# Second graph stream: late arrival of the last hidden state, and its next input normalised in two halves

## Chip, cores and metric

The kernel runs on one core of a Trainium2 chip. The metric is device time in microseconds (us) of one execution. Engines are named as in the profile: PE is TensorE's matmul, PEld its weight load, DVE is VectorE, ACT is ScalarE, POOL is GpSimd, SP is the queue that issues most DMAs.

## What is computed

The reference takes 16 graphs of 1024 nodes with 128 features each, a 0/1 adjacency per graph, and runs two residual blocks. The first block, where the change lies, is a gated graph network of 4 layers:

```python
h = relu(layernorm(x))
for i in range(4):
    m = einsum('bjn,bjd->bnd', adj, h @ weight[i])
    h = gru_cell(m, h, w_ih[i], w_hh[i], b_ih[i], b_hh[i])
x = x + h * mask
```

The second block is a 4-layer graph convolution with batch normalisation over `relu(layernorm(x))`. It is not touched.

## The kernel before

**Two streams.** The first block handles graphs in pairs: stream `sa` (the first stream) has the even graphs, stream `sb` (the second) the odd ones. While one stream sums over its adjacency, the other goes through its gates, so that PE always has matmuls. `half_step(one, two)` (L1032) is that unit: PE first does `two.gate_step(0)` and `two.gate_step(1)` (L955, the two halves of 512 nodes), then `one.agg_step(0)` and `one.agg_step(1)` (L525, 32 matmuls). Eight half-steps take a pair through a layer-by-layer cycle, and a loop (L1201) alternates `half_step(sa, sb)` and `half_step(sb, sa)`. `clock` counts them.

I number the half-steps of a cycle from the one in which `sb` finishes its graph:

| half-step | gates | aggregation |
|---|---|---|
| 0 | `sb`, layer 3 (then `sb` finishes) | `sa`, layer 0 of its next graph |
| 1 | `sa`, layer 0 | `sb`, layer 0 |
| 2 | `sb`, layer 0 | `sa`, layer 1 |
| 3 | `sa`, layer 1 | `sb`, layer 1 |
| 4 to 6 | and so on | |
| 7 | `sa`, layer 3 (then `sa` finishes) | `sb`, layer 3 |

**Gates.** For each half: six f32 matmuls into four PSUM tiles `g_r`, `g_hn`, `g_xn`, `g_z`, of which there is one set (so the second half may only write `g_z` after the first half's `z` has been read out); then on ACT sigmoid `r` (L981), tanh `r` (L987), sigmoid `z` (L988), and on DVE `r` (L982, L983) and the new `h` (L992 or L994, then L995, L996).

**Between layers.** The new `h` must come back turned (features by nodes to nodes by features). DVE turns 32x32 blocks (`t_h`, L711), SP writes them to DRAM (`cross_h`, L591, one DMA per half) and reads them back (`n_h`, L598, four DMAs per half). `split_back` (L898) then makes the aggregation's weights in two parts: ACT casts the high part `ghw` (L905, "hi" below, hi0 and hi1 for the halves) and DVE subtracts to get the low part (L906, "lo"). PE's aggregation wants hi0 first, lo0 two matmuls later, and hi1, lo1 only half-way.

**After a graph.** When a stream finishes (`finish`, L1001), the next graph's normalised input `y` takes the same road (`t_in`, `cross_in`, `h_in`), and so does the last `h` (`t_out`, `cross_out`, back into the two halves of `h`: `parts`, eight DMAs of L598). DVE then adds it to `x` and takes the sums of the layer norm (`tail_sums`, L717: L732, L658, L659). The next graph's `y` (`next_blocks`, L818) is made on ACT in eight blocks of 128 columns (L674, `y_in`).

**What sets the order.** Three engine orders are written by hand in this stage: PE, POOL and SP run in the order of the code. ACT and DVE are ordered by a scheduler that works with its own estimates, held by `behind(...)` (L761), which keeps instructions after named ones. Work that isn't of the current half-step is put on an agenda: `at(clock, place, what)` (L1025), run by `due(place)` (L1028). The place `"ins"` stands at the head of a half-step, `"outs"` between the two gate steps, `"gap"` between the two halves of the aggregation.

**The adjacency's transposes.** During the same cycle the adjacency blocks are transposed for the second block: POOL casts a row block to bf16 (L609, into two buffers), SP issues a DMA transpose (L610), a few per half-step (`feed.some`).

Of the kernel before, what the change touches and what calls it, by code (L numbers as in the profile page):

```python
# [8 lines left out]
F32 = mybir.dt.float32  # L9
# [7 lines left out]
P = 128  # L17
# [324 lines left out]
def exact_path(  # L342
# [22 lines left out]
    B, N, C = x.shape  # L365
    L = g_weight.shape[0]
    NB = N // P
    NH = N // HALF
    BH = HALF // P
# [28 lines left out]
    def turned_tile(name):  # L398
        return keep.tile([P, NB, N], BF16, tag="adjT", name=name, bufs=1)
# [134 lines left out]
    with ExitStack() as st:  # L534
        work = st.enter_context(tc.tile_pool(name="work", bufs=2))
# [58 lines left out]
        def exchange_in(d, t):  # L594

            src = d.rearrange("(t r) (s x) -> s r t x", t=4, s=4)
            for s in range(4):
                nc.sync.dma_start(t[s * 32 : (s + 1) * 32, :].rearrange("r (t x) -> r t x", t=4), src[s])  # L598
# [7 lines left out]
        def transpose_rows(b, row, j, adjT):  # L606

            t = work.tile([P, N], BF16, tag="half1", name=f"half{b}_{j}", bufs=2)
            nc.gpsimd.tensor_copy(t, row.bitcast(F32))  # L609
            return lambda: nc.sync.dma_start_transpose(adjT[:, :, j * P : (j + 1) * P], t)  # L610

        def transposes(batches):

            for b, rows in batches:
                adjT = turned_tile(f"adjT{b}")
                ahead = transpose_rows(b, rows[0], 0, adjT)
                for j in range(NB):
                    go = ahead
                    if j + 1 < NB:
                        ahead = transpose_rows(b, rows[j + 1], j + 1, adjT)  # L620
                    go()
                    yield j
                nc.gpsimd.dma_start(adjT_d[b].rearrange("k p n -> p k n"), adjT)
                yield NB
# [47 lines left out]
        def norm_blocks(xt, y, nt, ks):  # L672
            for k in ks:
                nc.scalar.activation(  # L674
                    y[:, k * P : (k + 1) * P], xt[:, k, :], AF.Relu, bias=nt[3][:, k, :], scale=nt[2][:, k, :]
                )
# [29 lines left out]
        def blocks_out(src, name):  # L706

            return [half_out(cross_tile(f"t_{name}_{hf}"), src, hf, name)[0] for hf in range(NH)]
# [39 lines left out]
        def last_tail(b, xt, hT):  # L748
            nt = tail_sums(b, xt, hT)
            y = y_mid(b) if b + 1 < B else xt.rearrange("p k c -> p (k c)")  # L750
            store_xmid(b, xt)

            def rest():
                norm_apply(xt, y, nt)
                store_ymid(b, y)

            return rest
# [3 lines left out]
        def behind(*inss):  # L761

            es = ExitStack()
            for ins in () if written[0] else inss:
                es.enter_context(tc.issue_after(ins.ins))
            return es

        class Stream:
# [47 lines left out]
                norm_factors(self.next_norm)  # L816

            def next_blocks(self):  # L818
                self.next_y = work.tile([P, N], F32, tag=f"y{self.tag}", name=f"y_in{self.b + 2}", bufs=1)
                norm_blocks(self.next_x, self.next_y, self.next_norm, range(NB))  # L820

            def plan(self, n, tail=None):

# [177 lines left out]
            def finish(self):  # L1001

                if self.i < L:
                    return
                args = self.b, self.xt, self.hT
                self.b, self.i = self.b + 2, 0
                if self.b >= B:
                    self.rest = last_tail(*args)
                    return
                ins = self.take()  # L1010
                h_in = self.hT
                outs = blocks_out(args[-1], f"out{args[0]}")
                parts = [args[-1][:, hf * HALF : (hf + 1) * HALF] for hf in range(NH)]

                def arrive(ds, ts):
                    for d, t in zip(ds, ts):
                        exchange_in(d, t)

                at(clock[0] + 1, "ins", lambda: arrive(ins, [h_in[:, :HALF], h_in[:, HALF:]]))
                at(clock[0] + 1, "outs", lambda: arrive(outs, parts))  # L1020
                self.plan(clock[0], (*args, parts))

        clock = [3]

        def at(n, place, go):  # L1025
            agenda.setdefault((n, place), []).append(go)

        def due(place):  # L1028
            for go in agenda.pop((clock[0], place), ()):
                go()  # L1030

        def half_step(one, two, gated=None, halfway=None):  # L1032

            feed.next_step()
            one.split = []
            if one.i == 0:
                two.fetch()
            due("ins")
            if one is sb and one.i == 0 or written[0] and one is sa:
                feed.jobs = transposes([(s.b, s.rows) for s in (sa, sb)])  # L1040
            if one.i > 0:
                one.split_step()
                two.fetch()
                feed.some(2)
            two.gate_step(0)
            two.half_away(0)
            two.first_four()
            if feed.full or (clock[0], "mid") in agenda:

                pace = small.tile([P, 1], F32, tag="pace", name=f"pace{clock[0]}")  # L1050
                nc.gpsimd.tensor_copy(pace, two.new[:, :1])
                feed.store()
                due("mid")
            due("outs")
            one.split_back(0, two.last_act, two.mid_dve)
            one.split_back(1, two.last_act, two.mid_dve)
            if one.i > 0:
                feed.some(1)
            two.gate_step(1, None, one.split)
            two.half_away(1)  # L1060
            with behind(two.first_act):
                due("late")
            if one.i == 0:
                feed.some(1)
            two.last_four()
            if gated:
                gated()
            if one.i == 0:
                with behind(two.last_m):
                    one.split_step()  # L1070
            one.agg_step(0)
            if halfway:
                halfway()
            with behind(two.last_act, two.last_dve, *one.split):
                due("gap")
            feed.some(NB if written[0] and one is sa else 1)
            one.agg_step(1)
            two.finish()
            clock[0] += 1

        sa, sb = Stream(0), Stream(1)
        every = {getattr(mybir.EngineType, e) for e in ("PE", "DVE", "Activation", "Pool", "SP")}
        with tc.tile_pool(name="prep", bufs=1) as prep, tc.manual_schedule(engines=every):
# [107 lines left out]
            sa.plan(0)  # L1191
            sb.plan(1)
            half_step(sa, sb, looks, lambda: turn_layer(prep, w_g, 1))
            join_layer(1)
            half_step(sb, sa, None, lambda: turn_layer(prep, w_g, 2))
            join_layer(2)
            turn_layer(prep, w_g, 3)
            join_layer(3)
        with tc.manual_schedule(engines={getattr(mybir.EngineType, e) for e in ("PE", "Pool", "SP")}):
            written[0] = False  # L1200
            for s in range(2, B // 2 * L):  # L1201
                half_step(sa, sb)
                half_step(sb, sa)
            assert not agenda, sorted(agenda)
            sb.gate_step(0)
            sb.gate_step(1)
            with tc.issue_after(sb.last_act.ins):
                sa.rest()
            sb.finish()
# [11 lines left out]
    work = ctx.enter_context(tc.tile_pool(name="work2", bufs=2))  # L1221
# [211 lines left out]
    for b in range(B):  # L1433
# [3 lines left out]
        for n0, n in pieces(b):  # L1437
# [3 lines left out]
            tag = turns[count % len(turns)]  # L1441
# [60 lines left out]
```

## Time and profile before

| | us |
|---|---|
| median of 3 runs (1797.73 to 1798.45) | 1797.83 |
| the profiled execution | 1797.0 |
| its span | 1795.1 |
| PE busy in the span | 1762.7 |
| granted TensorE clock, mean | 0.997 |

The span is what the profile shows; the 1.9 us beside it lie before and after. The first block takes the stretch from about 50 to 1160 us, the second the rest. PE is busy nearly everywhere, so what counts is where PE stands idle. The timeline of PE names each idle time of this stage with what ended it; the starts of the 32-matmul aggregations (L525) give the length of each half-step. Undisturbed, they start 17.57 us apart.

### The profile page before, as it was taken

To read this page: it belongs to the slowest core of one execution; us is meant where nothing else is said; L and a number is where in the kernel's file an instruction comes from. 1 tells how busy PE (TensorE), PEld (TensorE's weight loads), DVE (VectorE), ACT (ScalarE), POOL (GpSimd) and SP (SyncE) were. 2 spreads that over 40 slices of the span, in tenths; PEclk is the share of its full clock that TensorE was granted. 3 is DMA by queue.
4 is the path that set the end of the run, shared out by engine and by line. 5 is a ranking of instruction groups with operands and counts; after the bars stand their busy time and mean duration, and the time that the engine had idled before them with its cause. 6 is when DMAs were issued, how large, how long until landed. Compare 5 with 4: busy or idle time off the path is not lost.

```text
span 1795.1 us, 22286 instructions
## 1 busy us (share of the span) xinstructions
PE 1762.7 (98%) x6742; PEld 1194.2 (67%) x6742; DVE 1259.4 (70%) x2307; ACT 1108.3 (62%) x1717; POOL 389.0 (22%) x417
## 2 busy tenths in 40 slices
PE   9999999999999999999999999999999999999997
PEld 6555555565566555656555655677778888888886
DVE  7567867877776776877686766676666666666665
ACT  5346557466556555655655645477777767768765
POOL 3213423332332331422332333010100000000010
PEclk9999999999999999999999999999999999999999
DMA  6447777676676766766866767778866565757666
GB/s 252 113 127 263 190 206 245 197 214 212 213 208 217 230 192 196 255 201 175 284 175 187 246 197 211 270 270 309 280 220 246 205 247 207 255 214 251 230 227 255
DMA packets 363968, 399.11 MB, mean 222 GB/s; under 512 B 159820, under 2 KB 240496, under 8 KB 363840
## 3 DMA queue, kind: packets, MB, share of 16 engines
q1 hardware_dynamic: 343088, 322.54, 56.9%
q0 software_dynamic: 20224, 74.80, 11.5%
q8 instruction: 55, 0.90, 0.2%
q14 instruction: 73, 0.60, 0.1%
q10 hardware_dynamic: 528, 0.26, 0.0%
HBM read 266.95 MB, written 96.99 MB: 203 GB/s over the span
## 4 chain that ended last, share of the span: by engine, by line
PE 81%; DMA 5%; DVE 5%; ACT 4%; issue 2%; SPq 2%; DVEq 0%; ACTq 0%
PE pm L525 20%; PE pc_m L525 13%; PE g_z L969 10%; PE g_r L969 9%; PE pc_g_z L525 6%; PE pc_g_r L525 6%; PE g_xn L969 5%; PE g_hn L969 5%; PE hw_c L500 4%; DMA cross_in<-t_in 1%; ACT y_in L674 1%; SPq L598 1%; DMA stage<-in_adj_dram 1%; DMA cross_h<-t_h 1%; PE pw_g_hn L1302 1%
## 5 line engine op out<-in xcount | busy, mean ns | idle before, releaser
L525 PE MATMUL pm<-row,ghw 128*128 128x512 f32 x2048 | 505.3, 403 | 10.7 <-ACT ghw L905 10.6
L525 PEld LDWEIGHTS pm<-row,ghw 128*128 128x128 f32 x2048 | 384.3, 188 | 123.1 <-issue 26.3
L525 PE MATMUL pc_m<-wide,chw 128*128 128x512 f32 x1024 | 246.0, 395 | 0.0
L609 POOL CAST half<-row 128x1024 bf16<-128x1024 f32 x128 | 147.9, 1163 | 329.0 <-DMA adjT<-half 314.2
L525 PEld LDWEIGHTS pc_m<-wide,chw 128*128 128x128 f32 x1024 | 190.4, 188 | 42.3 <-issue 4.3
L988 ACT ACTIVATE z<-g_z,brz 128x512 f32<-128x512 f32 x128 | 87.5, 684 | 172.6 <-PE g_z L969 172.3
L525 PE MATMUL pc_g_r<-wide,chw 128*128 128x512 f32 x464 | 186.9, 403 | 0.3 <-ACT chw L502 0.3
L578 POOL CAST row<-stage 128x1024 fp32r<-128x1024 f32 x112 | 132.9, 1196 | 241.0 <-DMA stage<-in_adj_dram 194.9
L525 PE MATMUL pc_g_z<-wide,chw 128*128 128x512 f32 x464 | 181.0, 390 | 0.0
L982 DVE SCALAR_TENSOR_TENSOR r<-g_hn,vecs,r 128x512 f32<-128x512 f32 x128 | 95.1, 743 | 121.4 <-ACT r L981 76.6
L944 ACT COPY m<-pm 128x512 f32<-128x512 f32 x128 | 68.5, 587 | 151.6 <-PE pm L525 151.6
L1234 DVE CAST wide<-block 128x1024 fp32r<-128x1024 bf16 x160 | 109.9, 692 | 73.2 <-PE pc_m L525 48.3
L1234 DVE CAST wide<-packed 128x1024 fp32r<-128x1024 bf16 x160 | 110.2, 691 | 72.0 <-PE pc_g_z L525 53.9
L987 ACT ACTIVATE r<-r,vecs 128x512 f32<-128x512 f32 x128 | 91.8, 717 | 100.7 <-DVE r L983 100.5
L994 DVE TENSOR_TENSOR h<-h,r 128x512 f32<-128x512 f32 x96 | 81.3, 847 | 98.4 <-ACT r L987 98.4
L1232 ACT CAST wide<-packed 128x1024 fp32r<-128x1024 bf16 x96 | 100.6, 1048 | 59.0 <-PE pc_m L525 26.6
L969 PE MATMUL g_r<-m,w_mT 128*128 128x512 f32 x256 | 131.3, 594 | 3.5 <-ACT m L944 3.2
L1232 ACT CAST wide<-block 128x1024 fp32r<-128x1024 bf16 x96 | 100.6, 1048 | 52.3 <-PE pc_g_z L525 27.7
L969 PE MATMUL g_xn<-m,w_mT 128*128 128x512 f32 x256 | 130.7, 592 | 0.0
L969 PE MATMUL g_z<-m,w_mT 128*128 128x512 f32 x256 | 130.7, 592 | 0.0
L995 DVE TENSOR_TENSOR h<-h,z 128x512 f32<-128x512 f32 x128 | 116.3, 912 | 4.6 <-ACT z L988 1.5
L1282 DVE BATCH_NORM_STATS2 stats<-feat 128x6 f32<-128x512 f32 x128 | 84.1, 686 | 47.0 <-ACT feat L1281 45.9
(186 smaller groups left out, 2808.2 us busy)
## 6 DMA issues: line engine op xcount, KB each, us to landing
block<-adjT_d SPq DMA_DIRECT2D x256, 256.0 KB, 4.7
packed<-adjT_d SPq DMA_DIRECT2D x256, 256.0 KB, 5.6
stage<-in_adj_dram SPq DMA_DIRECT2D x120, 512.0 KB, 5.1
adjT_d<-adjT POOLq DMA_DIRECT2D x16, 2048.0 KB, 8.3
cross_h<-t_h SPq DMA_DIRECT2D x90, 256.0 KB, 3.0
n_h<-cross_h SPq DMA_DIRECT2D x360, 64.0 KB, 2.0
xmid_d<-x POOLq DMA_DIRECT2D x16, 512.0 KB, 5.3
y<-ymid_d POOLq DMA_DIRECT2D x16, 512.0 KB, 5.3
```

The source lines that it names most:

```text
L525: nc.tensor.matmul(pm[hf], hw[s][:, j * P : (j + 1) * P], rows[j][:, hf * HALF : (hf + 1) * HALF], start=(j == 0 and s == 0), stop=(j == N ...
L578: nc.gpsimd.tensor_copy(t, stage[j % 4])
L609: nc.gpsimd.tensor_copy(t, row.bitcast(F32))
L969: nc.tensor.matmul(po, wT[:, i, g * C : (g + 1) * C], rhs, start=start, stop=stop)
L982: nc.vector.scalar_tensor_tensor(r, phn, b_hn(i), r, ALU.add, ALU.mult)
L987: nc.scalar.activation(r, r, AF.Tanh, bias=b_in(i))
L988: self.last_act = nc.scalar.activation(z, pz, AF.Sigmoid, bias=brz[:, 3 * i + 1 : 3 * i + 2])
L994: nc.vector.tensor_sub(ho, hin, r)
L995: nc.vector.tensor_mul(ho, ho, z)
L1232: nc.scalar.copy(r, t)
L1234: nc.vector.tensor_copy(r, t)
L1282: nc.vector.bn_stats(stats[:, b * NH + hf, :], dst)
```

## The change

It does three things, all in the first block's loop.

1. The place `"outs"` (the eight DMAs that bring back a finished graph's last `h`) moves. Before, it stood between the gate steps, after `half_away(0)`. Now it stands, in half-steps with `one is sa`, behind `one.split_step()` and `two.fetch()` and ahead of `feed.some(2)`.
2. For `sb` these DMAs are due two half-steps after the finish instead of one: half-step 2 instead of 1. For `sa` they stay in half-step 0. (A second `due("outs")` for `one is sb` finds nothing on the agenda.)
3. `sb`'s eight blocks of the next `y` were all in the gap of half-step 7. Now four are, and the other four are put in the next half-step 0 at a new place, `"behind m"`, where `behind(two.last_m)` holds them after the copies `m` (L944) of the aggregation's result.

```diff
             def next_blocks(self):
-                self.next_y = work.tile([P, N], F32, tag=f"y{self.tag}", name=f"y_in{self.b + 2}", bufs=1)
-                norm_blocks(self.next_x, self.next_y, self.next_norm, range(NB))
+                y = work.tile([P, N], F32, tag=f"y{self.tag}", name=f"y_in{self.b + 2}", bufs=1)
+                args = self.next_x, y, self.next_norm
+                self.next_y = y
+                if self is sa:
+                    norm_blocks(*args, range(NB))
+                    return
+                norm_blocks(*args, range(BH))
+                at(clock[0] + 1, "behind m", lambda: norm_blocks(*args, range(BH, NB)))
...
                 at(clock[0] + 1, "ins", lambda: arrive(ins, [h_in[:, :HALF], h_in[:, HALF:]]))
-                at(clock[0] + 1, "outs", lambda: arrive(outs, parts))
+                at(clock[0] + (1 if self is sa else 2), "outs", lambda: arrive(outs, parts))
...
             if one is sb and one.i == 0 or written[0] and one is sa:
                 feed.jobs = transposes([(s.b, s.rows) for s in (sa, sb)])
+            with behind(two.last_m):
+                due("behind m")
             if one.i > 0:
                 one.split_step()
                 two.fetch()
+            if one is sa:
+                due("outs")
+            if one.i > 0:
                 feed.some(2)
             two.gate_step(0)
+            if one is sb:
+                due("outs")
             two.half_away(0)
...
                 due("mid")
-            due("outs")
             one.split_back(0, two.last_act, two.mid_dve)
```

Since a scheduler orders ACT and DVE, the order of the built program is part of the change. On PE and POOL the changed program has the same order as before. On SP only the eight `h<-cross_out` DMAs of `sb` move, once per cycle. On ACT and DVE, the same hunks recur in each of the seven cycles (hi and lo as above, `z` and `r` of the second gate half):

| half-step | ACT before | ACT after |
|---|---|---|
| 7 to 0 | `y_in` x8, `m`, `m`, hi x2 of `sa`, `r` | `y_in` x4, `m`, `m`, `y_in` x4, `r`, hi x2 of `sa` |
| 2 | `z`, hi0, hi1, tanh | hi0, `z`, hi1, tanh |
| 3 | hi0, `r`, hi1, `z` | `r`, `z`, hi0, hi1 |
| 4 | hi0, hi1, `r`, `z` | hi0, `r`, hi1, `z` |

On DVE, in half-step 0 the order `low`, lo0, `low`, L982, lo1, L983, `t_in`, `t_in` becomes `low`, `t_in`, `low`, L982, lo0, L983, lo1, `t_in`; in half-step 2 the order up to lo0 stays the same (L992, L995, L982, L996, L983, `t_h`, lo0, lo1), and the eight L732 of `sb`'s tail are taken four and four; in half-step 3 lo0 and lo1 move from beside L995 to behind `t_h`.

## Prediction

> **What bounds the kernel now.** The page's first part comes first, then PE's timeline over the first block, where every idle time names what ended it.
>
> ```profile
> PE 1762.7 (98%) x6742; PEld 1194.2 (67%) x6742; DVE 1259.4 (70%) x2307; ACT 1108.3 (62%) x1717; POOL 389.0 (22%) x417
> ...
> 364.05 7.83 PE L525 MATMUL pm<-row,ghw 128*128 128x512 f32 x32
> ...
> 346.47 7.85 PE L525 MATMUL pm<-row,ghw 128*128 128x512 f32 x32 [1.28 <-ACT ghw L905]
> 444.01 1.12 PE L969 MATMUL g_r<-m,w_mT 128*128 128x512 f32 x2 [0.97 <-ACT m L944]
> 1064.12 9.46 PE L525 MATMUL pm<-row,ghw 128*128 128x512 f32 x32 [2.85 <-ACT ghw L905]
> ```
>
> PE is the bound; only its stalls can give time. An aggregation that waits for nothing shows no bracket. The starts of the aggregations give what a stall really costs, against 17.57 us undisturbed. Two places lose, each once per cycle, seven times:
>
> Place B, half-step 2 (346.47 above): 1.85 or 1.86 us in each of six cycles (19.42 or 19.43 between starts); in the last cycle 3.41 and, through the second half of the weights, another 1.63 (20.98 and 19.20), so 5.04.
>
> Place A, half-step 0 (444.01 above): by cycle 0.27, 1.24, 1.43, 0.40, 0.54, 0 and 1.43, together 5.31.
>
> With B's 6 x 1.86 + 5.04 = 16.2, the two hold 21.5 us. That is the most that the change could take away.
>
> **Part 1, the late `outs` (place B).** The SP, ACT and DVE timelines of that half-step:
>
> ```profile
> 333.91 4.62 SPq L598 DMA_DIRECT2D h<-cross_out  x8
> 338.62 0.38 SPq L591 DMA_DIRECT2D cross_h<-t_h  x1
> 339.11 2.66 SPq L610 DMA_TRANSPOSE adjT<-half  x2
> 341.82 3.90 SPq L598 DMA_DIRECT2D n_h<-cross_h  x8
> ...
> 345.22 0.69 ACT L988 ACTIVATE z<-g_z,brz 128x512 f32<-128x512 f32 x1 [2.75 <-PE g_z L969]
> 345.81 0.61 ACT L905 CAST ghw<-n_h 128x512 fp32r<-128x512 f32 x1
> ...
> 342.18 1.41 DVE L995 TENSOR_TENSOR h<-h,z 128x512 f32<-128x512 f32 x1
> 345.55 0.70 DVE L711 STREAM_TRANSPOSE t_h<-h 128x512 f32<-128x512 f32 x1
> 346.44 0.69 DVE L906 TENSOR_TENSOR ghw<-n_h,ghw 128x512 fp32r<-128x512 f32 x1 [0.20 <-ACT ghw L905]
> ...
> 342.00 1.05 POOL L609 CAST half<-row 128x1024 bf16<-128x1024 f32 x1 [10.92 <-DMA adjT<-half]
> ```
>
> The eight `outs` take SP 4.6 us and push everything behind them: the second `cross_h` (its `t_h` ended at 334.04), two transposes, then `n_h`. The gates of half-step 2 end on PE at G = 345.19. ACT takes hi0 only behind `z`, which waits for G itself; hi0 is ready at 346.42, and lo0 ends at 347.13, G + 1.94. The third matmul needs lo0. The loss is lo0's end less G, less 0.08 (1.94 gives 1.86).
>
> Afterwards `n_h` starts 4.6 us sooner, near 337.2, and its first half lands near 341.1 (two transposes 2.66, four issues of 0.48, about 2.0 to land). ACT has hi0 ahead of `z`, behind the sigmoid `r` that ends at 342.5: ready at 343.1. So hi0 no longer waits, and **what is late next is lo0**, which keeps its place on DVE behind L992, L995, L982, L996, L983 and `t_h`. L992 starts at 341.45, behind tanh, which is behind `z` of the first half: nothing here moves it. L995 took 1.41 at 342.18, under POOL's cast; undisturbed, as at 379.62, it takes 0.69, and such steps start 0.60 to 0.66 apart. The casts wait for the transposes, which also come 4.6 us sooner, so the casts move to about 337.4 to 339.9, where DVE reads PSUM (L982, L983: 0.75 and 0.69 beside a cast at 325) or takes layer-norm sums, which kept 0.26 beside a cast at 357. So lo0 starts five steps of 0.62 behind 342.18, at 345.28, and ends at 345.97, G + 0.78. Loss 0.70, gain 1.16; six cycles give 7.0.
>
> The last cycle: there DVE is late by itself (L982 at 1056.61, behind a tail that began late), and ACT's hi0 at 1063.45 waited 1.45 for `n_h`. With `n_h` early, lo0 follows `t_h` (1062.34, 0.17 sooner without the cast) and ends near 1063.5, G = 1061.27 plus 2.2. Loss 2.1 in place of 5.04, gain 2.9. **B gives 9.9.**
>
> The `outs` themselves come to stand behind `n_h`, at about 341.1 to 345.7; they land by 347.7, and `sb`'s tail reads them at 353.6 before (near 351 after). The two transposes behind them are issued at 345.7, against 345.81 before. So they cost nothing, with 3 us to spare. For `sa`, no transposes are queued in half-step 0, so its SP order is unchanged: 0.
>
> [...] By the row, the casts cost this chain 0.72 in L995 and 0.17 in L996. [...]
>
> **Part 1's price (place C, half-step 3).** The scheduler also moved ACT's casts here. Before:
>
> ```profile
> 360.90 0.60 ACT L905 CAST ghw<-n_h 128x512 fp32r<-128x512 f32 x1
> 361.41 0.68 ACT L981 ACTIVATE r<-g_r,brz 128x512 f32<-128x512 f32 x1
> 361.99 0.60 ACT L905 CAST ghw<-n_h 128x512 fp32r<-128x512 f32 x1
> 364.65 0.69 ACT L988 ACTIVATE z<-g_z,brz 128x512 f32<-128x512 f32 x1 [2.06 <-PE g_z L969]
> ```
>
> hi0 ran in ACT's pause before `z`; PE started at 364.05 without a bracket. Afterwards both casts stand behind `z`, which waits for the last gate matmul. That is exactly the order that place B had before. `z` 364.65, hi0 365.24 to 365.84, lo0 (DVE is free by then) to 366.55: G = 364.61 plus 1.94. So the same loss, 1.86, appears in seven half-steps that lost nothing: **+13.0.** Queued behind these casts on ACT are tanh (0.3 later) and `y_mid`, then the next `m`, which had 0.95 us to spare and gains 1.86 with PE's delay. Half-step 4 moves only hi1, needed half an aggregation later: 0.
>
> **Part 2, `y` in two halves (place A).**
>
> ```profile
> 440.31 3.17 ACT L674 ACTIVATE y_in<-x,ms_in,rs_in 128x128 f32<-128x128 f32 x8
> 443.39 1.04 ACT L944 COPY m<-pm 128x512 f32<-128x512 f32 x2
> 450.58 0.72 ACT L987 ACTIVATE r<-r,vecs 128x512 f32<-128x512 f32 x1 [4.52 <-DVE r L983]
> 451.20 0.67 ACT L988 ACTIVATE z<-g_z,brz 128x512 f32<-128x512 f32 x1
> ```
>
> The aggregation ends at E = 442.07. With four blocks ACT is free at 441.9, just when `m` can start, and the stall at `m` is gone. But look at the 4.52: tanh waits for DVE, which is behind its `low` reductions, and `z` stands behind tanh until 451.87. PE may write the second half's `g_z` only then; without the stall it comes there at E + 8.59 = 450.66. Even in time by 0.13, that hand-over cost 0.19 in this cycle, so I count `z`'s end + 0.32 less E + 8.59. That is 1.53 where `m` cost 1.43: the stall just moves. By cycle: 0.25, 0.91, 1.53, 0, 0.64, 0, 1.53, sum 4.86 against 5.31. **A gives 0.4.** The four blocks behind `m` delay sigmoid `r` to about 444.5 and its end to 445.1; DVE's L982, which reads it, starts at 448.60 whatever happens, and on DVE the same work stands ahead of L983. Cost 0; if the reductions were short, the delay would be 0.7 us, still inside the 5.15 us of a gate half.
>
> **Sum.** +13.0 - 9.9 - 0.4 = +2.7. The profiled execution took 1797.0 (span 1795.1 and 1.9 around it), so 1799.7; it lies 0.83 under the median shown, and beside the median that is **1800.5 us**. From run to run this kernel can tell about 0.2%, 3.6 us, from no change; 2.7 is inside.
>
> **Rivals.** (1) Slower: the casts stay on DVE's chain. If the two transposes are issued later than about 338.5 (a landing of 2.9 then puts a cast on L992 or L995), lo0 ends at 346.96, only 0.17 sooner than before, so B gives 6 x 0.17 and perhaps 1.6 in the last cycle, 2.6; C still costs 13.0: +10, about 1807.8. For: DVE's 1.41 recurs in all cycles at this place. Against: SP has nothing else queued there. (2) Faster: B recovers all 16.2, if DVE is not late, and A between 0.4 and 5.3, if `low` is not late: -3.6 to -8.5, about 1792. For: cycles 4 and 6 have `z` early enough. Against: lo0's place on DVE. (3) C doesn't bite, because it only replaces a wait: B and A alone give -10.3, 1787.5. Against: 364.65 starts 0.04 after the last gate matmul, and ACT has no way past it. (4) The change does nothing, since PE's order is the same: 1797.8; but the orders on ACT and SP differ in every cycle.
>
> **Numbers.** Forecast 0.55 (mostly within 0.2%, its upper edge above); rival 1 0.27; rival 2 0.11; rivals 3 and 4 0.07. A's bounds (a loss of 1 to a gain of 5.3) and B's (2.6 to 16.2) stretch the forecast's own range to 1796 to 1805. To leave out no more than 2 in 10, the range reaches rival 1: 1795.0 to 1808. Faster 0.10, within 0.2% 0.53, slower 0.37.
>
> **What would show it.** Right: in the changed profile, half-step 2's aggregation has a bracket no longer put down to L905 and starts about 18.3 after its forerunner; half-step 3's has [1.28 <-ACT ghw L905] and 19.43; `m`'s bracket is gone and `g_z` of half-step 0 waits for `z` in cycles 2, 3, 5 and 7. Wrong: no bracket at half-step 3 (then C fails, and the kernel is faster by about 10), 1.41 still on L995 in half-step 2 (then rival 1), or half-step 0 without any stall (then A gives up to 5.3).

## The result and the profile after

The changed kernel takes **1805.08 us** (median of 6 runs, 1802.85 to 1807.11), beside 1798.14 for the kernel before in the same session. The ratio is 1.0042, with the interval [1.003, 1.0054]: slower by about 7 us. The profiled execution took 1805.76 us, its span is 1803.9. The range of the prediction holds the time; its likeliest case (no change that can be told) was not the one that came.

Lines of the changed kernel's code are shifted: L905 is now L911, L906 is L912, L982 is L988, L988 is L994, L995 is L1001. In the kernels of the experiments some lines shift by a few more; there the names of the tiles tell which step it is.

From the page after, the busy times, and the group of the first block's aggregation. Its last column is PE's idle time ahead of these matmuls.

```profile
PE 1766.7 (98%) x6742; PEld 1193.6 (66%) x6742; DVE 1259.5 (70%) x2307; ACT 1107.3 (61%) x1717; POOL 378.6 (21%) x417
...
L525 PE MATMUL pm<-row,ghw 128*128 128x512 f32 x2048 | 508.8, 404 | 16.9 <-ACT ghw L911 9.0
```

The same group in the page before:

```profile
L525 PE MATMUL pm<-row,ghw 128*128 128x512 f32 x2048 | 505.3, 403 | 10.7 <-ACT ghw L905 10.6
```

PE's timeline after, half-steps 2 and 3 of the second cycle, half-step 0 of the third, and half-step 3 of the fourth:

```profile
343.81 1.03 PE L525 MATMUL pm<-row,ghw 128*128 128x512 f32 x2
345.17 7.11 PE L525 MATMUL pm<-row,ghw 128*128 128x512 f32 x30 [0.33 <-DVE ghw L912]
...
363.87 0.73 PE L525 MATMUL pm<-row,ghw 128*128 128x512 f32 x2 [1.28 <-ACT ghw L911]
365.18 7.11 PE L525 MATMUL pm<-row,ghw 128*128 128x512 f32 x30 [0.59 <-DVE ghw L912]
...
449.95 1.13 PE L975 MATMUL g_hn<-h,w_hhT 128*128 128x512 f32 x2 [0.50 <-DVE r L988]
452.48 1.12 PE L975 MATMUL g_z<-h,w_hhT 128*128 128x512 f32 x2 [0.20 <-ACT z L994]
...
652.16 0.73 PE L525 MATMUL pm<-row,ghw 128*128 128x512 f32 x2 [1.28 <-ACT ghw L911]
654.81 9.93 PE L525 MATMUL pm<-row,ghw 128*128 128x512 f32 x30 [1.92 <-DVE ghw L912]
```

Place B (345.17) now waits for DVE's lo0, and only 0.33. Place C (363.87) waits 1.28 for hi0, as predicted, and then once more for lo0, which was not. Place A (449.95) no longer waits for `m`. And the 30 matmuls at 654.81 take 9.93 where they took 7.11 at 365.18.

PE's busy time grew by 4.0 with the same 6742 instructions: 3.5 of it in this group, whose matmuls are the same in number and shape. About 2.0 of that is only how an aggregation in two pieces is counted. The two pieces at 343.81 and 345.17 are busy for 8.14 in place of the undisturbed 7.84, and so in each of the seven cycles; the 0.33 that the bracket shows there and these 0.30 are one loss of 0.63. Most of the rest is longer matmuls, which no wait explains: the pieces at 652.16 and 654.81 are busy for 10.66, 2.8 more than 7.84. The kernel before has one such aggregation, at 1064.12, with 1.6 more.

What each place loses is best taken from the ends of successive aggregations less 17.575. By cycle, after: A 0, 0.7, 1.6, 0, 1.4, 1.4, 1.6; B 0.6 six times, then 2.0; C 1.8, 2.4, 1.8, 6.6, 2.5, 2.8, 1.8. The sums stand in the table with those of the experiments (one profiled execution each). One column holds parts of the losses already counted: the number of half-steps (in A, B or C) with a stretch at half clock, and the time by which their aggregations ran longer than 7.85 for it.

| kernel | A | B | C | half-clock half-steps, us | time (median) | ratio to before |
|---|---|---|---|---|---|---|
| before | 5.4 | 16.2 | 0 | 1, 1.6 | 1797.4 to 1798.1 by session | |
| after | 6.7 | 5.7 | 19.8 | 1, 2.8 | 1805.08 | 1.0042 [1.003, 1.0054] |
| part 1 alone | 6.5 | 6.5 | 22.8 | 3, 4.7 | 1809.67 | 1.0066 [1.0052, 1.008] |
| part 2 alone | 2.6 | 19.1 | 0 | 2, 3.0 | 1796.63 | 0.9993 [0.9984, 1.0002] |
| after, `z` held | 4.9 | 5.8 | 6.3 | 0 | 1792.04 | 0.9965 [0.9951, 0.9978] |
| after, casts late | 3.2 | 5.4 | 12.9 | 0 | 1795.82 | 0.9991 [0.9982, 1.0] |
| before, `z` held | 6.5 | 14.9 | 0 | 1, 1.3 | 1796.54 | 0.999 [0.9981, 0.9999] |
| part 1, `z` held | 7.0 | 5.9 | 5.5 | 0 | 1792.45 | 0.9968 [0.9956, 0.998] |
| after, `z` held, casts late | 2.0 | 5.5 | 4.1 | 0 | 1786.28 | 0.9936 [0.9923, 0.995] |
| after, splits ahead of `r` | 4.2 | 1.0 | 0.6 | 0 | 1783.49 | 0.9919 [0.9906, 0.9933] |
| the same, casts late | 2.4 | 1.2 | 0.8 | 0 | 1780.79 | 0.9902 [0.9885, 0.9918] |
| the same, `y` in one piece | 4.5 | 0.9 | 0.4 | 0 | 1782.07 | 0.9908 [0.9892, 0.9925] |
| part 1, casts late | 3.4 | 5.3 | 12.9 | 0 | 1797.06 | 0.9996 [0.9987, 1.0005] |

From before to after: A +1.3, B -10.5, C +19.8, together 10.7. Ahead of the first full cycle, the changed kernel is 0.6 sooner, and its second block is 1.4 shorter; that leaves the 8.8 between the spans.

**Place B, after** (SP, ACT, DVE):

```profile
337.84 3.85 SPq L598 DMA_DIRECT2D n_h<-cross_h  x8
...
341.57 0.61 ACT L911 CAST ghw<-n_h 128x512 fp32r<-128x512 f32 x1
344.41 0.69 ACT L994 ACTIVATE z<-g_z,brz 128x512 f32<-128x512 f32 x1 [2.24 <-PE g_z L975]
...
341.38 0.69 DVE L1001 TENSOR_TENSOR h<-h,z 128x512 f32<-128x512 f32 x1
...
344.47 0.65 DVE L912 TENSOR_TENSOR ghw<-n_h,ghw 128x512 fp32r<-128x512 f32 x1
```

`n_h` is issued from 337.84 (before: 341.82), hi0 runs 2.8 us ahead of `z`, L1001 takes 0.69 in place of 1.41, and lo0 alone is late.

**Place C, after**: ACT, DVE and POOL in the second cycle (from 362.62), the fourth (from 652.14) and the seventh (from 1093.38):

```profile
362.62 0.69 ACT L994 ACTIVATE z<-g_z,brz 128x512 f32<-128x512 f32 x1 [2.69 <-PE g_z L975]
363.21 1.13 ACT L911 CAST ghw<-n_h 128x512 fp32r<-128x512 f32 x2
...
363.85 1.28 DVE L912 TENSOR_TENSOR ghw<-n_h,ghw 128x512 fp32r<-128x512 f32 x1 [1.08 <-ACT ghw L911]
...
363.92 0.89 POOL L743 DMA_DIRECT2D xmid_d<-x  x1
364.80 2.66 POOL L609 CAST half<-row 128x1024 bf16<-128x1024 f32 x2
...
652.14 2.60 DVE L912 TENSOR_TENSOR ghw<-n_h,ghw 128x512 fp32r<-128x512 f32 x1 [1.08 <-ACT ghw L911]
...
652.17 2.02 POOL L609 CAST half<-row 128x1024 bf16<-128x1024 f32 x2
...
1093.38 0.69 DVE L912 TENSOR_TENSOR ghw<-n_h,ghw 128x512 fp32r<-128x512 f32 x1 [1.08 <-ACT ghw L911]
...
1093.38 0.89 POOL L623 DMA_DIRECT2D adjT_d<-adjT  x1 [2.04 <-DMA adjT<-half]
```

lo0 takes 0.65 at place B. Here it takes 1.28 in the second cycle, beside POOL's issue of a DMA and the first of its two row casts, and 2.60 in the fourth, beside both casts. In the fourth cycle the casts take 2.02, as two do at 338.58 with no lo0 beside them, and DVE alone is held; in the second the two casts take 2.66. In the seventh, lo0 lies beside the issue of a DMA alone and takes 0.69. The traces tell which of POOL's steps counts. Between 150 and 1165 us of the 13 profiles, 196 of the DVE steps that write `h` or lo lay beside a DMA issue of POOL and no cast, and took 0.65 to 0.70; all 1201 of them that took longer than 0.8 overlapped a cast. So it is the casts, and not the issues, that go with a longer step.

**The clock.** The windows views after and before; the third column from the right is the granted clock.

```profile
648.00:652.00 4.00, 2.88 (x7) 0.95 (x5) 3.06 (x5) 1.31 (x3) 1.77 (x3) 1.00 0.19 46
652.00:656.00 4.00, 1.92 (x5) 1.30 (x6) 3.82 (x4) 4.00 (x11) 2.20 (x3) 0.75 1.02 397
656.00:660.00 4.00, 4.00 (x11) 3.13 (x10) 2.34 (x5) 1.92 (x3) 0.00 (x0) 0.50 0.99 390
```

```profile
1066.00:1070.00 4.00, 4.00 (x13) 3.11 (x12) 3.83 (x5) 2.25 (x4) 3.28 (x4) 0.61 0.70 167
```

From 654.0 to 660.9 the clock is 0.5. That is the 9.93. In the kernel before, it is 0.5 from 1065.7 to 1069.1, behind the 2.85 that PE waited at 1064.12: the last cycle's second 1.63 was clock, not a late half of the weights.

### The profile page after: what moved, and what is told of

Read it like the earlier page. It is cut to its first block, busy times and chain, and to the rows that moved or that the text cites. A ratio compares the mean times of both kernels' runs of the same rounds, so it can differ in the third digit from the quotient of the medians.

```text
span 1803.9 us, 22307 instructions
## 1 busy us (share of the span) xinstructions
PE 1766.7 (98%) x6742; PEld 1193.6 (66%) x6742; DVE 1259.5 (70%) x2307; ACT 1107.3 (61%) x1717; POOL 378.6 (21%) x417
## 4 chain that ended last, share of the span: by engine, by line
PE 74%; DVE 8%; DMA 6%; SPq 5%; ACT 3%; issue 3%; POOL 0%; DVEq 0%; ACTq 0%; POOLq 0%
PE pm L525 18%; PE pc_m L525 13%; PE g_z L975 8%; PE g_r L975 8%; PE pc_g_z L525 6%; PE pc_g_r L525 6%; PE hw_c L500 4%; PE g_hn L975 4%; PE g_xn L975 4%; SPq L598 3%; DMA stage<-in_adj_dram 2%; DVE low L604 2%; DVE h L1002 1%; DVE h L1001 1%; DMA cross_h<-t_h 1%
## 5 line engine op out<-in xcount | busy, mean ns | idle before, releaser
L525 PE MATMUL pm<-row,ghw 128*128 128x512 f32 x2048 | 508.8, 404 | 16.9 <-ACT ghw L911 9.0
L609 POOL CAST half<-row 128x1024 bf16<-128x1024 f32 x128 | 144.2, 1134 | 322.6 <-DMA adjT<-half 307.9
L994 ACT ACTIVATE z<-g_z,brz 128x512 f32<-128x512 f32 x128 | 87.5, 684 | 176.0 <-PE g_z L975 175.8
L988 DVE SCALAR_TENSOR_TENSOR r<-g_hn,vecs,r 128x512 f32<-128x512 f32 x128 | 95.0, 742 | 135.8 <-ACT r L987 88.1
L578 POOL CAST row<-stage 128x1024 fp32r<-128x1024 f32 x112 | 129.1, 1161 | 250.0 <-DMA stage<-in_adj_dram 229.9
L1000 DVE TENSOR_TENSOR h<-h,r 128x512 f32<-128x512 f32 x96 | 79.7, 830 | 95.8 <-ACT r L993 95.8
L1002 DVE TENSOR_TENSOR h<-h,r 128x512 f32<-128x512 f32 x128 | 111.4, 874 | 2.3
```

The costliest lines, as they stand in the source:

```text
L525: nc.tensor.matmul(pm[hf], hw[s][:, j * P : (j + 1) * P], rows[j][:, hf * HALF : (hf + 1) * HALF], start=(j == 0 and s == 0), stop=(j == N ...
L578: nc.gpsimd.tensor_copy(t, stage[j % 4])
L988: nc.vector.scalar_tensor_tensor(r, phn, b_hn(i), r, ALU.add, ALU.mult)
L994: self.last_act = nc.scalar.activation(z, pz, AF.Sigmoid, bias=brz[:, 3 * i + 1 : 3 * i + 2])
L1000: nc.vector.tensor_sub(ho, hin, r)
L1002: self.last_dve = nc.vector.tensor_add(ho, ho, r)
```

## The experiments

My theory was that the cost is place C, made of three layers: hi0 behind `z` (1.84 per cycle, 12.9), lo0 held beside POOL's casts (brackets of 0.59, 1.92, 0.62 and 0.94 in four of the seven cycles, 4.1) and the half clock behind the longest such stall (2.8): 19.8. The rivals: the moved DMAs or `y` in two halves cost by themselves; or, of the layers, only one matters.

### Each part alone

Part 1 alone: `y` in one piece again.

```diff
-                if self is sa:
-                    norm_blocks(*args, range(NB))
-                    return
-                norm_blocks(*args, range(BH))
-                at(clock[0] + 1, "behind m", lambda: norm_blocks(*args, range(BH, NB)))
+                norm_blocks(*args, range(NB))
```

> The changed kernel with its second part undone: y of the second stream in one piece of eight blocks, the outs moved as in the change. Theory (the loss sits in half-step 3, where ACT's order puts hi0 behind z, and lo0 on DVE runs into POOL's casts): in the changed profile half-step 0 lost 6.7 us over seven cycles against 5.4 before, so this kernel takes about 1.3 us less than the changed one, near 1803.7, still 5 to 6 us over the kernel before; half-step 3 keeps its bracket of 1.28 put down to the cast hi0. Rival (the second part is what costs, by its four blocks behind m): at or below the kernel before, near 1796.

It took 1809.67, 4.6 more than both parts: a miss. Part 2 helps beside part 1. Half-step 3 of cycle 5 on PE, and lo0 in cycle 4 on DVE:

```profile
802.42 0.72 PE L525 MATMUL pm<-row,ghw 128*128 128x512 f32 x2 [1.28 <-ACT ghw L907]
803.52 8.70 PE L525 MATMUL pm<-row,ghw 128*128 128x512 f32 x30 [0.37 <-DVE ghw L908]
```

```profile
653.67 3.23 DVE L908 TENSOR_TENSOR ghw<-n_h,ghw 128x512 fp32r<-128x512 f32 x1 [0.45 <-ACT ghw L907]
```

Three aggregations ran partly at half clock (4.7 us longer for it, in place of 2.8), and lo0 was held for longer (brackets of 5.1 in place of 4.1). That makes the 3.0 more at C. The last run below tests it.

Part 2 alone: the `outs` as before.

```diff
-                at(clock[0] + (1 if self is sa else 2), "outs", lambda: arrive(outs, parts))
+                at(clock[0] + 1, "outs", lambda: arrive(outs, parts))
...
-            if one is sa:
-                due("outs")
-            if one.i > 0:
...
-            if one is sb:
-                due("outs")
...
                 due("mid")
+            due("outs")
```

> The kernel before with only the second part of the change: y of the second stream in two halves, the outs where they were. Theory: the stall at m goes and comes back at g_z, behind DVE's reductions; within -0.4 and +1.3 us of the kernel before, 1797.7 to 1799.4, and half-step 3 without a bracket. Rival (the second part costs): some 6 us over the kernel before, near 1804.

1796.63: by its interval no difference, and 1 us below what was expected. A fell to 2.6. B is 19.1 in place of 16.2: a second stretch at half clock makes 1.4 of that, and the other 1.6, spread over the cycles, was not explained. C stayed at 0. So part 2 does not make the kernel slower; part 1 does.

### The order on ACT, and POOL's casts, each alone

`z` of the second gate half is held behind the split's ACT casts (`after[:1]` is hi1, and hi0 is ahead of it).

```diff
-                self.last_act = nc.scalar.activation(z, pz, AF.Sigmoid, bias=...)
+                with behind(*after[:1]):
+                    self.last_act = nc.scalar.activation(z, pz, AF.Sigmoid, bias=...)
```

> The changed kernel with one hold more: ACT's sigmoid z of the second gate half stays behind the casts hi0 and hi1 in every half-step, so that hi0 no longer waits for the last gate matmul in half-step 3; DVE's and SP's orders stay those of the change. Theory: in half-step 3 only lo0's place behind t_h remains, a loss near 0.7 us as in half-step 2, in place of 1.84 to 6.58; seven cycles go from 19.8 to about 4.9, so some 15 us under the changed kernel: near 1790, under the kernel before by 8. Rival (the outs ahead of the transposes on SP make the data late, and ACT's order only follows it): the loss in half-step 3 stays, bracket put down to a DMA, 1805 or more.

1792.04, 2 us above what was expected, and far under the rival's 1805. Only ACT's order differs from that of the changed kernel; PE, DVE and POOL run in the same order. ACT, PE and DVE at place C, second cycle:

```profile
359.29 1.13 ACT L911 CAST ghw<-n_h 128x512 fp32r<-128x512 f32 x2
361.63 0.72 ACT L993 ACTIVATE r<-r,vecs 128x512 f32<-128x512 f32 x1 [1.22 <-DVE r L989]
362.26 0.67 ACT L995 ACTIVATE z<-g_z,brz 128x512 f32<-128x512 f32 x1
...
363.71 7.09 PE L525 MATMUL pm<-row,ghw 128*128 128x512 f32 x30 [1.21 <-DVE ghw L912]
...
362.14 1.51 DVE L912 TENSOR_TENSOR ghw<-n_h,ghw 128x512 fp32r<-128x512 f32 x1
```

ACT's casts start 2.7 us ahead of the end of the gates on PE, in place of 0.6 behind it, and what is left is lo0: 0.6 by its place behind `t_h`, and 0.9 more in the two cycles in which a cast of POOL overlaps it. C falls by 13.5 to 6.3. One order of two instructions is worth 13 us here.

In the other, POOL's `pace` (a one-column copy that holds back the two DMA issues and the casts) reads lo1 where there is one, in place of `h`, and comes after `split_back` in the code.

```diff
+            one.split_back(0, two.last_act, two.mid_dve)
+            one.split_back(1, two.last_act, two.mid_dve)
             if feed.full or (clock[0], "mid") in agenda:
                 pace = small.tile([P, 1], F32, tag="pace", name=f"pace{clock[0]}")
-                nc.gpsimd.tensor_copy(pace, two.new[:, :1])
+                src = one.hw[1][:, HALF : HALF + 1].bitcast(F32) if one.split else two.new[:, :1]
+                nc.gpsimd.tensor_copy(pace, src)
                 feed.store()
                 due("mid")
-            one.split_back(0, two.last_act, two.mid_dve)
-            one.split_back(1, two.last_act, two.mid_dve)
```

> The changed kernel with POOL's pacing copy made to wait for lo1 on DVE in place of the new h, so that POOL's casts of half-step 3 start behind lo0 and lo1; ACT's, DVE's and SP's orders are those of the change. Theory: of the 19.8 us lost in half-step 3, 13.0 come from ACT's order and stay (bracket 1.28, loss 1.84 in each cycle); the 3.4 from lo0 beside POOL's casts and the 3.4 from the half clock that follows the longest of these stalls go: near 1798, about the kernel before. Rival (the casts have nothing to do with it; lo0 is late for another reason): 1805, losses between 1.84 and 3 as in the change.

1795.82, 2 us under what was expected. ACT, DVE and PE run in the same order as in the changed kernel. PE, DVE and POOL at place C:

```profile
364.03 7.83 PE L525 MATMUL pm<-row,ghw 128*128 128x512 f32 x32 [1.28 <-ACT ghw L911]
...
364.01 1.29 DVE L912 TENSOR_TENSOR ghw<-n_h,ghw 128x512 fp32r<-128x512 f32 x2 [1.15 <-ACT ghw L911]
...
365.37 0.58 POOL L1067 COPY pace<-ghw 128x1 f32<-128x1 f32 x1 [8.34 <-DVE ghw L912]
```

hi0 still waits behind `z` (1.28), but lo0 and lo1 take 1.29 together, and the 32 matmuls run in one piece. C is 1.84 in every cycle, 12.9, where the prediction had 13.0. The first block has no stretch at half clock any more. The three places lose 21.5 in all, against 21.6 before, and the time is where the forecast had it: no change that can be told. That is not C's doing alone. Beside the changed kernel, A lost 3.5 less as well, and why was not tested; with the 6.7 that A lost there, the sum would be 25.0.

### The hold without the moved DMAs, and the layers together

> The kernel before with only the hold: z of the second half behind hi0, the outs where they were. In half-step 2 of before, hi0 stood behind z at 345.81 us, but its n_h was issued from 341.82 us only. Theory (the outs ahead of n_h on SP and the order on ACT are two covers of one delay, and either alone keeps it): hi0 still waits for n_h, half-step 2 loses 1.5 to 1.9 as before, 1795.5 to 1798.5. Rival (the order on ACT was the whole cause, the outs need not have moved): half-step 2 falls to 0.6 to 0.7 per cycle, about 1787 to 1789.

The same hold of `z` in the kernel before: 1796.54, as the theory had it. SP and ACT at place B:

```profile
342.74 3.89 SPq L598 DMA_DIRECT2D n_h<-cross_h  x8
...
346.39 0.62 ACT L905 CAST ghw<-n_h 128x512 fp32r<-128x512 f32 x1 [4.00 <-DMA n_h<-cross_h]
```

hi0 now stands ahead of `z` and waits for `n_h`. So at place B of before there were two delays, one behind the other: the order on ACT, and the `outs` ahead of `n_h` on SP. Taking away the order alone brings almost nothing. The other half, the moved `outs` with hi0 still behind `z`, was not run at place B; at place C, where nothing but that order holds hi0 in the run with late casts, it costs 1.84.

> Part 1 with the second half's sigmoid z held behind hi0, and the coming y in one piece again. In the run that had part 1 alone, half-step 3 lost 22.8 us, and three half-clock windows of 3.41 us (about 1.7 us each) fell into it. Theory: those windows follow from half-step 3's two stalls in a row, so without the stall behind z they go as well, and part 2 is worth under 2 us: 1790 to 1794, no half-clock window in the first block. Rival: y in one piece beside the moved outs costs its 4.6 us by itself, at m in half-step 0: 1796 to 1797.

Part 1 with the hold: 1792.45, within 0.5 of both parts with the hold (1792.04). With C's stalls short, no half-clock window came, and beside the hold `y` in halves is worth nothing that can be measured.

> The changed kernel with both: z held behind hi0, and POOL's row casts paced behind lo1. With the hold alone half-step 3 lost 6.3 us in seven cycles (1.49 and 1.55 in the two cycles where the casts lay on lo0, 0.62 to 0.67 elsewhere); with the casts moved alone half-step 0 lost 3.2 in place of 4.9. Theory: the two causes add up, half-step 3 loses 0.62 seven times (4.4), half-step 0 about 3.2: 1787 to 1790. Rival: with hi0 early the casts no longer matter, and pacing them later only delays the row transposes: 1792 or more.

Hold and late casts together: 1786.28, 0.7 under the expected range. Each brings something beside the other (9.5 and 5.8 us), but together, 18.8 under the changed kernel, less than the 13.0 and 9.3 that they bring alone. C is 0.56 to 0.70 in each cycle.

The next step takes hi0 ahead of the second half's sigmoid `r` and lo0 ahead of DVE's step that reads `g_hn`. (`split` now keeps hi1, lo1, hi0, lo0.)

```diff
                         self.split = [
                             nc.scalar.copy(hi, back),
                             nc.vector.tensor_sub(lo, back, hi.bitcast(F32)),
+                            *self.split,
                         ]
...
-                self.first_act = nc.scalar.activation(r, pr, AF.Sigmoid, ...)
-                nc.vector.scalar_tensor_tensor(r, phn, b_hn(i), r, ALU.add, ALU.mult)
+                with behind(*after[2:3]):
+                    self.first_act = nc.scalar.activation(r, pr, AF.Sigmoid, ...)
+                with behind(*after[3:]):
+                    nc.vector.scalar_tensor_tensor(r, phn, b_hn(i), r, ALU.add, ALU.mult)
...
-                with behind(*after[1:]):
+                with behind(*after[1:2]):
```

> The hold taken one step further: hi0 also ahead of the second half's sigmoid r on ACT, and lo0 ahead of the r step that reads g_hn on DVE. What is left of the stalls in half-steps 2 and 3 with the hold (5.8 and 6.3 us) is lo0 standing behind six DVE steps. Theory: both go to nearly nothing, half-step 0 stays at 4.9: a gain of 10 to 12 on the hold's 1792.0, that is 1779 to 1783. Rival: the gate chain, now 0.6 us later on ACT and 0.7 on DVE, ends too late for the next use of its accumulators or for h, and the stall moves there: 1786 or more.

1783.49, half a us above the expected range, and well under the rival's. PE at places B and C, and the page's group of these matmuls:

```profile
341.96 7.83 PE L525 MATMUL pm<-row,ghw 128*128 128x512 f32 x32
359.54 7.84 PE L525 MATMUL pm<-row,ghw 128*128 128x512 f32 x32
```

```profile
L525 PE MATMUL pm<-row,ghw 128*128 128x512 f32 x2048 | 504.4, 403 | 1.8 <-DVE ghw L912 1.0
```

No bracket, 17.58 apart; PE's idle time ahead of them fell from 16.9 to 1.8. The gate chain, 0.6 later, made nobody wait at these two places; half-step 0 still loses 4.2.

> All three together: hi0 and lo0 ahead of the second half's r, z behind hi1, and POOL's row casts paced behind lo1. With the splits early, half-steps 2 and 3 lost 0.98 and 0.64 us in all, so the casts no longer lie on them; half-step 0 lost 4.2 with the casts where they were, and 2.0 to 3.2 in the two runs that had them paced later. Theory (the two edits act on different half-steps and add up): another 1 to 2.5 us, 1780.5 to 1782.5 beside the 1783.5 of the run without the pace. Rival: the pace is now held by lo1, which the early split moves to 1.6 us earlier, so the casts come to lie elsewhere, and nothing is gained: 1783 to 1785.

With the late casts as well: **1780.79**, the fastest of all, 1% under the kernel before. That it beats the run without the pace (1783.49) is likely and not certain: the runs of the two overlap.

> The same kernel with the coming y in one piece, so that part 2 is measured where no other stall hides it. Theory (with y in one piece, half-step 0 lost 5.4, 6.4, 6.5 and 7.0 us in four runs; with y in two halves and the casts paced later, 2.0 and 3.2): 3 to 5 us slower than with y in two halves. Rival (the stall at m and the one at z are each the other's cover, as the prediction had it): within 1 us of it.

The same with `y` in one piece: 1782.07. A is 4.5 in place of 2.4, but the runs overlap, so the 3 to 5 us expected were a miss; part 2 is worth 1 or 2 us here, if anything.

> Part 1 alone (y in one piece, the order r, z, hi0, hi1 left as it is) with POOL's row casts paced behind lo1. Part 1 alone took 1809.7, 4.6 more than both parts; its half-step 3 lost 22.8 us. Theory: that surplus is lo0 held under POOL's casts and the half-clock windows that follow such pairs of stalls; with the casts away half-step 3 loses 7 times 1.84, 12.9, no half-clock window is left in the first block, and the time is that of both parts with the same pace (1795.8) plus at most 2: 1795.5 to 1798. Rival: y in one piece costs its 4.6 wherever hi0 stands behind z, casts or not: 1800 to 1801.

Part 1 with the late casts and the order on ACT left alone: 1797.06, as expected, against 1795.82 with both parts. C is 12.9 again, and no half-clock window came. So of the 4.6 that part 1 alone lost against both parts, 3.4 go when the casts come late, and 1.2 stay. Why `y` in one piece lets the casts hold lo0 longer was not found, and of the 5.0 us between the two profiled executions C has only 3.0.

## Why the prediction was right or wrong

**B, right.** -9.9 forecast, -10.5 measured. lo0 became the late one, at a loss of 0.61 to 0.65 where 0.70 was worked out; the last cycle lost 2.0 for a forecast of 2.1. One row was misread: the last cycle's 1.63 was half clock. The sum held: PE waited 2.85 ahead of that half clock before and 1.69 at the same place after, where the granted clock stayed at 1.00 (1064 to 1080).

**A, right in mechanism, and 1.7 off.** -0.4 forecast, +1.3 measured. The stall did move from `m` to the second half's gates. But it waited first for DVE's `r` (0.34 to 0.50) and then 0.20 for `z`, and cycles 5 and 6 lost 1.4 each where 0.6 and 0 were forecast. In the other runs with `y` in halves A lay between 2.0 and 4.9, so 6.7 may be partly this execution's; those runs differ in other things as well.

**C, the step that failed: "lo0 (DVE is free by then) to 366.55: G = 364.61 plus 1.94", and with it +13.0.** The wait behind `z` was right to the tenth: 1.84 seven times, 12.9, seen alone in the run with late casts. DVE was free, too: it stood idle for 1.08 ahead of lo0. What failed is the time of lo0 itself, 0.71 in that sum, about what it takes with no cast beside it (0.65 at place B, 0.69 in the seventh cycle). Behind `t_h`, lo0 falls into the stretch of POOL's two DMA issues and two row casts, which POOL starts once `h` of the first gate half is there and, in five of the seven cycles, once a transpose (`adjT<-half`) has landed, 0.67 to 2.04 later. In four cycles lo0 took 1.28 to 2.60. That cost 4.1 more, and the half clock behind the longest stall 2.8: 19.8 for 13.0. The prediction had seen DVE's L995 take 1.41 beside POOL's casts and 0.69 without, and used it at place B; it did not ask what POOL does at the place where lo0 would come to stand. Nor was 1.41, one step beside one cast and the first 0.20 of the next, the longest step beside casts: lo0 took 2.60, and the profile before already had a step of 2.16 beside two casts (L994 of the kernel before, at 653.49).

By what mechanism the casts hold DVE was not shown; the traces give lengths and order. At 652.14 lo0 outlasted both casts, and they took no longer than 2.02. By the records lo0 started 0.03 ahead of the first cast and was held all the same. In the second cycle both sides were stretched (lo0 1.28, the two casts 2.66). At place B, with no cast of POOL from 340.65 (L998) to 345.12, lo0 ended 0.75 behind G (345.12 and 344.37), where the prediction had 0.78.

**The sum.** 10.7 in place of 2.7 in the first block, less 1.9 elsewhere. The time came near that of rival 1 (1807.8), but not by its mechanism: there lo0 was to stay late at B under the casts, and B gave its 10.5. The forecast's own range ended at 1805; that the wider range holds 1805.08 is owed to the edge that this rival set, and so to luck. Rival 3 (C does not bite) is refuted by [1.28 <-ACT ghw L911] in all seven cycles.

## What to carry to other kernels

When an edit makes an instruction later, list what the other engines do at its new place: the price of a moved step is not only its wait, but whom it meets. Where two delays stand one behind the other (here a DMA queue and an engine's order), taking away one may show nothing: the hold alone brought under 2 us, and beside the moved `outs` 13. And where a scheduler orders an engine, state the order that you need: holding one sigmoid behind the casts turned this change from 0.42% slower into 0.35% faster, and two more holds with a later pace into 1% faster.

## What the hardware showed

Short stalls cost twice here. By the recorded changes of the clock in the first block, it stood at 0.5 for 3.41 us at a time, once for 6.83. The changes lie whole multiples of 3.4133 us apart (190, 2 and 333 of them in the profile after; 310, 1 and 211 in the one before). I cut each profile into such windows and added up PE's idle time in each that ran at full clock, over the part of the first block that the table covers. Every window with 1.8 us or more of idle (seven: 1.82, 1.95, 1.96, 2.23, 2.41, 2.69, 2.91) was followed by half clock; of those with 1.5 to 1.7, one (1.66) was and seven were not. So in this stage a window with 1.82 us or more of idle time cost another 1.3 to 1.6 us for each 3.41 at half clock (the column of the table). No single wait in the loop was longer than 2.91. Whether two stalls fall into one window is partly chance: behind the same two brackets, 1.28 and 0.94, the 30 matmuls took 8.72 in part 1 alone (at 950.33) and 7.11 in the changed kernel (at 948.15), where one window held 1.64 of the idle time. In the second block two windows with only 1.31 us of recorded idle time were followed by half clock too, so the 1.8 is what this stage showed and no more. The ends of matmuls are modelled, and some records can be missing.
